# A second DMA queue for h and for zeros and scales, and a rank for bank copies, in a fused int4 FFN and S4 convolution kernel

## The chip, the cores and the metric

The kernel runs on one core of a Trainium2 chip. The metric is the device time of one execution in microseconds. Before the change three runs gave a median of 1330.53 us (1329.95 to 1332.14). The views quoted come from one profiled execution, which took 1331.74 us; its span, from the first instruction to the last, is 1330.0 us.

Engines are named as in the profile: PE multiplies matrices (PEld is its weight load), DVE and ACT work on vectors, POOL is the fourth compute engine, and SP here only issues transfers. SPq and POOLq are the queues in which those two engines hold their transfers: an engine takes its instructions in order, and an instruction that waits holds all behind it.

## The reference

x is 2048 x 1024. It is normalised row by row to xn, and the output is x plus two branches of xn:

```
xn  = (x - mean) / sqrt(var + 1e-5)
y   = irfft(rfft(xn, 2L) * rfft(K, 2L))[:L] + D * xn     # a causal convolution, L = 1024
g, u = xn @ Wg.T, xn @ Wu.T                              # 2752 columns each
h   = silu(g) * u
out = x + y + h @ Wd.T
```

Wg, Wu and Wd are held as 4-bit values, two to a byte, with a scale and a zero for each group of 64 along the input: w = (q - zero) * scale. K is the kernel of a state space model with 64 states, computed from its coefficients.

## The kernel before

All products are made in fp16 pairs: a float32 value is split into a high and a low half, and three of the four products of halves are taken. On top of that, the FFN uses a seven-product scheme in place of eight for a 2 x 2 block product: sums and differences of blocks are formed first, seven block products are made, and results are combined.

**First part (to about 145 us).** The rows are loaded, normalised, turned and combined; weights for the first column tiles are prepared by hand order (`pin`).

**Gate/up loop (about 145 to 875 us).** j runs over column tiles of 128 (j from 2 to 20 here), cp over two halves of the rows; `gate_up(j, cp, ...)` is one *unit*. A unit is seven products of 12 matmuls each into four PSUM banks A, B, C and D. Between products a bank's contents are copied or added on. ACT copies A to B (line 619), C to hb, B to D and C to ha, and makes the two silus; DVE adds D to hb and B to ha, and multiplies ha and hb by the silus. Three of the seven products of a unit (`fifth`, `fourth`, `third`, kept in `pending`) run inside the next unit. Tags limit buffers: banks A and C share four, B and D have two each, h tiles have four each for even j and for odd j.

`finish_h` stores h to DRAM (HF) as seven sums: of an even j it stores ha and keeps both halves; of the following odd j it stores both halves and forms and stores s4, s2, s5 (in s0's place) and s6. Each store is 256 KB, by SP. For the last j, h is split into halves and sent to HPL, from where the second stage reads it.

In the same loop weights are made ready, and this work is traced ahead of a unit or between units:

- `load_w` (two granules for each j, prepared a j ahead): raw values and scales by SP; unpack on DVE; `scale_c` (line 320), three short POOL operations on the scales; 16 ACTIVATEs on ACT that apply scale and zero; four sums on DVE (`sums`); high halves on ACT, low halves on DVE (both `nat`); two transposing transfers into `wf`, issued by SP (`w_t`, line 403). `wf` has four buffers, two for each j.
- `load_wd` (line 461), a generator that is stepped four times after every unit: the down weights, in ten rounds u of two granules ga and gb. `fetch_wd` loads raw values, spreads the transposed zeros and scales (SZT) over a factor tile `w` of two buffers by four transfers of 64 partitions each on SP (line 480), and has the raw values transposed. `dequant` (line 489) subtracts and multiplies on DVE; sums, high halves and low halves (`nd`) follow, and SP stores them to WD.

What orders the work: the Tile framework's planner orders each engine's instructions when the kernel is built. It simulates the program with its own durations, and among the instructions that are ready in the simulation it takes the one traced first; `tc.high_priority(n)` lets what is traced in its block count as if traced n instructions earlier. `tc.issue_after(ins)` puts what is traced in its block behind `ins` on the same engine. `tails` holds one DVE instruction for each finished unit, and `lag` counts them; the first dequant of a round is put behind the last of them (line 519), the second (line 533) is not. On the chip the order is fixed: an engine that waits for a late transfer doesn't pass on to the next instruction.

**Second stage (from about 875 us).** The convolution's products, and then the down product from HF and WD, whose results are added into the output by accumulating transfers from POOL's queue (line 1261).

Of the kernel before, what the change touches and what calls it, by code (L numbers as in the profile page):

```python
# [24 lines left out]
F16 = mybir.dt.float16  # L25
# [4 lines left out]
ALU = mybir.AluOpType  # L30
# [3 lines left out]
P = 128  # L34
# [4 lines left out]
NJ = 21  # L39
N_GRAN = 2 * NJ + 1 + 2 * NPAIR + 2  # L40
G_MIX = 2 * NJ
G_WD = G_MIX + 1
# [12 lines left out]
HS = 4.0  # L55
# [32 lines left out]
def build(nc, tc, x, xp, raw_d, sz_d, par_d, vct_d, tab_d, csrow_d, out):  # L88
# [3 lines left out]
    with es:  # L92
# [8 lines left out]
        HF = [dr.tile([7, P, NPAIR, 512], F32, name=f"HF{c}") for c in range(2)]  # L101
        HPL = [dr.tile([P, 2, 3, 512], F16, name=f"HPL{c}") for c in range(2)]
        WD2 = [dr.tile([7, P, NPAIR // 2, 2, 2, P], F16, name=f"WD{m}") for m in range(1, 8)]
        SZT = dr.tile([2 * NPAIR, 2, 2, 8, P], F32, name="SZT")
# [3 lines left out]
        def htile(name, tag="h"):  # L108
            return pools["h"].tile([P, 512], F32, tag=tag, name=name)
# [28 lines left out]
        def wtemp(kind, shape, dtype, name):  # L138
            return home[kind].tile(shape, dtype, tag=kind, name=name, **({"bufs": szbufs[0]} if kind == "sz" else {}))
# [14 lines left out]
        def split(dst, src):  # L154

            A.copy(dst[:, 0], src)
            V.tensor_tensor(dst[:, 1], src, dst[:, 0], ALU.subtract)
# [130 lines left out]
        with ea:  # L288
# [172 lines left out]
            def load_wd(u):  # L461


                pr, kq = divmod(u, 2)
                ga, gb = (G_WD + 2 * p + kq for p in (pr, pr + NPAIR // 2))
                tt, sub = V.tensor_tensor, ALU.subtract

                def load(gi):
                    raw = rawd[gi] = wtemp("raw", [P, 16, 32], I32, f"raw{gi}")
                    SP.dma_start(raw, raw_d[gi].rearrange("p (a b) -> p a b", a=16))  # L470

                def fetch_wd(gi):


                    raw = rawd.pop(gi)
                    w = wtemp("wd", [P, 8, 256], F32, f"w{gi}")
                    for i in range(2):
                        for b in range(2):
                            SP.dma_start(w[64 * b : 64 * b + 64, 4 * i : 4 * i + 4].rearrange("p f c -> p (f c)"),
                                         SZT[gi - G_WD, 1 - i, b].rearrange("c h -> (c h)").partition_broadcast(64))  # L480
                    q = wtemp("raw", [P, 16, 2, 32], I16, f"qn{gi}")
                    low = raw.bitcast(I16).rearrange("p a (b c) -> p a b c", c=2)[:, :, :, 0]
                    V.tensor_scalar(q[:, :, 0, :], low, 4, 15, ALU.logical_shift_right, ALU.bitwise_and)
                    V.tensor_scalar(q[:, :, 1, :], low, 15, None, ALU.bitwise_and)
                    qt = raw.bitcast(I16).rearrange("p a b -> p (a b)").rearrange("p (a b) -> p a b", a=8)
                    SP.dma_start_transpose(qt, q.rearrange("p a b c -> p (a b c)"))
                    return w, qt

                def dequant(w, qt):
                    x4 = w[:, 0:4]  # L490
                    tt(x4, qt.rearrange("p (f a) b -> p f (a b)", f=4), x4, sub)
                    tt(x4, x4, w[:, 4:8], ALU.mult)

                blocks = lambda w: w.rearrange("p f (m c) -> p f m c", m=2)
                nats = {}

                def hi(i, src):
                    nats[i] = wtemp("nat", [P, 7, 2, P], F16, f"nd{u}_{i}")
                    A.copy(nats[i][:, :, 0], src)

                def lo(i, src):
                    nat = nats.pop(i)
                    tt(nat[:, :, 1], src, nat[:, :, 0], sub)
                    SP.dma_start(
                        WD2[i - 1][:, :, pr, kq].rearrange("f p a c -> p f (a c)"), nat.rearrange("p f a c -> p f (a c)")
                    )

                nxt = [G_WD + 2 * ((u + 1) // 2 + o) + (u + 1) % 2 for o in (0, NPAIR // 2)] if u + 1 < NPAIR else None
                if u == 0:
                    load(ga)  # L510
                    load(gb)
                    yield from lag()
                    ready_wd[ga] = fetch_wd(ga)
                    yield
                ready_wd[gb] = fetch_wd(gb)
                yield from lag(2 if u == 0 else 1)
                ma = ready_wd.pop(ga)
                with tc.issue_after(tails[-1].ins):
                    dequant(*ma)
                wa = blocks(ma[0][:, 0:7])  # L520
                yield
                sums(ma[0], True)
                hi(1, wa[:, :, 0])
                yield
                if nxt:
                    load(nxt[0])
                lo(1, wa[:, :, 0])
                tt(wa[:, :, 0], wa[:, :, 1], wa[:, :, 0], sub)
                hi(5, wa[:, :, 0])
                yield  # L530
                lo(5, wa[:, :, 0])
                mb = ready_wd.pop(gb)
                dequant(*mb)
                wb = blocks(mb[0][:, 0:7])
                yield
                sums(mb[0], True)
                hi(3, wb[:, :, 1])
                tt(wa[:, :, 1], wb[:, :, 1], wa[:, :, 1], sub)
                yield
                if nxt:  # L540
                    load(nxt[1])
                lo(3, wb[:, :, 1])
                hi(7, wa[:, :, 1])
                tt(wb[:, :, 1], wb[:, :, 1], wa[:, :, 0], sub)
                yield

                lo(7, wa[:, :, 1])
                hi(6, wb[:, :, 1])
                if nxt:
                    ready_wd[nxt[0]] = fetch_wd(nxt[0])  # L550
                yield
                hi(2, wb[:, :, 0])
                lo(6, wb[:, :, 1])
                yield
                lo(2, wb[:, :, 0])
                tt(wb[:, :, 0], wb[:, :, 0], wb[:, :, 1], sub)
                hi(4, wb[:, :, 0])
                yield
                lo(4, wb[:, :, 0])
                yield  # L560
# [33 lines left out]

            pending = []

            def gate_up(j, cp, wf):

                def prod(i, ps, start, stop):
# [16 lines left out]
                add, mult = ALU.add, ALU.mult  # L616
                bA, bB = bank("A" + nm), bank("B" + nm, "B")
                prod(1, bA, True, True)
                heads[j, cp] = A.copy(bB, bA)
                rest(0)  # L620
                bC = bank("C" + nm)
                prod(7, bC, True, True)
                tag = "h" if j % 2 else "e"
                hb = htile("hb_" + nm, tag)
                A.copy(hb, bC)
                rest(1)
                prod(6, bB, False, True)
                bD = bank("D" + nm, "D")
                A.copy(bD, bB)
                prod(2, bA, False, True)  # L630
                A.activation(bA, bA, AF.Silu, scale=isc)
                rest(2)

                def fifth():
                    prod(5, bD, False, True)
                    tails.append(V.tensor_tensor(hb, bD, hb, add))

                def fourth():
                    prod(4, bC, False, True)
                    ha = htile("ha_" + nm, tag)  # L640
                    A.copy(ha, bC)
                    V.tensor_tensor(ha, bB, ha, add)
                    V.scalar_tensor_tensor(ha, ha, HS * isc, bA, mult, mult)
                    pending[2] = lambda: third(ha)

                def third(ha):
                    prod(3, bD, False, True)
                    A.activation(bD, bD, AF.Silu, scale=isc)
                    V.scalar_tensor_tensor(hb, hb, HS * isc, bD, mult, mult)
                    finish_h(j, cp, ha, hb)  # L650

                pending[:] = [fifth, fourth, None]

# [16 lines left out]
                V.scalar_tensor_tensor(h, bu, HS * isc, h, ALU.mult, ALU.mult)  # L670
                return h

            def finish_h(j, cp, ha, hb):
                nm = f"{j}_{cp}"
                if j == NJ - 1:
                    for c, h in enumerate((ha, hb)):
                        pc = wtemp("nat", [P, 2, 512], F16, f"hpl{nm}_{c}")
                        split(pc, h)
                        A.dma_start(HPL[cp][:, c, 0:2, :], pc)
                    return  # L680
                def emit(f, src):
                    SP.dma_start(HF[cp][f, :, j // 2, :], src)

                if j % 2 == 0:
                    emit(0, ha)
                    slots[cp] = (ha, hb)
                    return
                s0, s2 = slots.pop(cp)
                s1, s3 = ha, hb
                s4, s6 = (htile(f"s{n}_{nm}") for n in (4, 6))  # L690
                emit(1, s1)
                emit(3, s3)
                V.tensor_tensor(s4, s0, s2, ALU.subtract)
                emit(4, s4)
                V.tensor_tensor(s2, s2, s3, ALU.add)
                emit(2, s2)
                V.tensor_tensor(s0, s2, s0, ALU.subtract)
                emit(5, s0)
                V.tensor_tensor(s6, s1, s0, ALU.subtract)
                emit(6, s6)  # L700


            s4p = cst.tile([P, 208], F32, name="s4p")
# [705 lines left out]
```

## Time and profile before

| What | us |
|---|---|
| median of three runs | 1330.53 |
| profiled execution | 1331.74 |
| its span | 1330.0 |
| PE busy | 1274.0 |
| DVE busy | 987.9 |
| ACT busy | 669.2 |
| POOL busy | 182.8 |

Busy PE counts matmuls whose ends are modelled, 512 columns being issued every 0.216 us at full clock. In a group's row the numbers after the bar are busy time, mean ns of one, and the engine's idle time just before them with what ended it. In the list of waits the numbers are total us, how many waits, and the longest. A window's row gives busy times in a stretch and the clock that the throttle granted PE.

### The profile page before, as it was taken

Reading aid. Unit: us, or ns where it says so; the run is one execution under the profiler, and the core shown is the slowest. Engines: PE = TensorE matmul, PEld = TensorE weight load, DVE = VectorE, ACT = ScalarE, POOL = GpSimd, SP = SyncE. Lnnn points to the kernel's source line nnn. Section 1 sums busy time; section 2 is a strip of 40 time slices with the busy share of each in tenths; the row PEclk is TensorE's granted clock in tenths of the full one; section 3 lists DMA queues with packets and bytes.
Section 4 is the critical chain, followed back from the end, with each engine's and each line's share of the span. In section 5 each row is a group of like instructions: output and inputs, shape, how many; then the busy total and the mean of one; then the engine's idle time right before and its main releaser. Section 6 shows DMA issues by size and latency. Waiting matters only on the chain. (4 is left out here: it accounts for less than half of the span.)

```text
span 1330.0 us, 20904 instructions
## 1 busy us (share of the span) xinstructions
PE 1274.0 (96%) x7880; PEld 751.9 (57%) x7880; DVE 987.9 (74%) x1344; ACT 669.2 (50%) x1208; POOL 182.8 (14%) x267
## 2 busy tenths in 40 slices
PE   5999899999999899989989998999999999999998
PEld 5644344444444344444444443456558888888887
DVE  6779967486886877786878777462738898779792
ACT  4867566656656474766568475420204433443330
POOL 3230001010100000000111000000000032256440
PEclk8999899999999999999999998999999999999999
DMA  6791958469887988888798887765837779799981
GB/s 225 173 218 31 196 152 186 97 163 251 212 229 159 240 217 207 223 210 232 191 264 224 216 215 180 216 213 187 333 122 292 273 202 265 238 262 274 285 181 48
DMA packets 358401, 276.04 MB, mean 208 GB/s; under 512 B 211668, under 2 KB 304668, under 8 KB 354204
## 3 DMA queue, kind: packets, MB, share of 16 engines
q1 hardware_dynamic: 335676, 261.59, 70.6%
q0 software_dynamic: 21760, 10.49, 6.6%
q10 hardware_dynamic: 864, 2.62, 0.5%
q8 instruction: 62, 1.02, 0.3%
q14 instruction: 39, 0.32, 0.1%
HBM read 132.36 MB, written 94.84 MB: 171 GB/s over the span
## 5 line engine op out<-in xcount | busy, mean ns | idle before, releaser
L77 PEld LDWEIGHTS <-wf 128*128 128x128 f16 x3960 | 375.7, 99 | 467.8 <-issue 45.2
L77 PEld LDWEIGHTS <-g 128*128 128x128 f16 x2940 | 287.6, 98 | 33.5 <-issue 0.2
L77 ACT ACTIVATE w<-w,sz 128x64 f32<-128x64 int32 x640 | 217.9, 427 | 74.9 <-DVE w L77 58.3
L77 PE MATMUL A<-x,wf 128*128 128x512 f16 x912 | 215.2, 385 | 13.4 <-ACT ha L77 5.3
L77 PE MATMUL D<-x,wf 128*128 128x512 f16 x912 | 211.5, 380 | 14.1 <-DVE hb L77 12.1
L77 PE MATMUL C<-x,wf 128*128 128x512 f16 x912 | 208.0, 381 | 2.8 <-DVE ha L77 2.6
L77 ACT CAST g<-a 128x2560 f16<-128x2560 f32 x42 | 97.5, 2324 | 182.1 <-PE cv L77 52.6
L77 PE MATMUL A<-b,g 128*128 128x256 f16 x1680 | 185.9, 273 | 0.0
L77 DVE TENSOR_TENSOR w<-w 128x256 f32<-128x256 f32 (+2 forms) x272 | 136.9, 527 | 61.2 <-ACT w L77 54.7
L77 DVE TENSOR_TENSOR g<-a,g 128x2560 f16<-128x2560 f32 x42 | 118.4, 2821 | 30.9 <-ACT g L77 30.9
L1261 POOL DMA_DIRECT2D out<-o x64 | 78.8, 2139 | 360.7 <-DVE o L77 348.2
L322 POOL TENSOR_SCALAR sz<-sz 128x16 f32<-128x16 f32 x42 | 18.6, 443 | 673.2 <-DMA sz<-in_sz 622.7
L77 PE MATMUL B<-x,wf 128*128 128x512 f16 x456 | 106.7, 384 | 1.8 <-ACT B L77 1.8
L77 ACT CAST nat<-w 128x896 f16<-128x896 f32 x76 | 68.3, 935 | 72.9 <-issue 34.4
L77 ACT CAST nd<-w 128x896 f16<-128x896 f32 x70 | 64.1, 933 | 68.9 <-DVE w L77 47.6
L77 DVE TENSOR_TENSOR nat<-w,nat 128x896 f16<-128x896 f32 x76 | 81.0, 1087 | 19.3 <-ACT nat L77 19.1
L77 PE MATMUL D<-b,g 128*128 128x256 f16 x840 | 94.0, 273 | 0.0
L77 DVE TENSOR_TENSOR nd<-w,nd 128x896 f16<-128x896 f32 x70 | 75.5, 1086 | 16.3 <-ACT nd L77 16.0
L77 PEld LDWEIGHTS <-x 128*128 128x128 f16 x576 | 52.4, 98 | 23.7 <-issue 2.7
L77 DVE SCALAR_TENSOR_TENSOR p<-cv,p 128x512 f32<-128x512 f32 x32 | 21.9, 688 | 50.3 <-PE cv L77 44.9
L77 PE MATMUL cv<-band,x 128*128 128x512 f16 (+3 forms) x384 | 57.1, 299 | 0.0
L77 PE MATMUL g<-x,wf 128*128 128x128 f16 (+1 forms) x336 | 48.8, 293 | 1.7 <-ACT wf L82 0.8
(145 smaller groups left out, 1203.8 us busy)
## 6 DMA issues: line engine op xcount, KB each, us to landing
a<-HF SPq DMA_DIRECT2D x28, 1280.0 KB, 8.1
WD<-nd SPq DMA_DIRECT2D x70, 448.0 KB, 4.4
b<-WD SPq DMA_DIRECT2D x49, 640.0 KB, 5.9
w<-SZT SPq DMA_DIRECT2D x80, 256.0 KB, 5.7
raw<-in_raw SPq DMA_DIRECT2D x65, 256.0 KB, 3.8
HF<-ha SPq DMA_DIRECT2D x54, 256.0 KB, 2.9
HF<-s SPq DMA_DIRECT2D x40, 256.0 KB, 3.0
HF<-hb SPq DMA_DIRECT2D x36, 256.0 KB, 3.6
```

The lines of the kernel that those rows point to most:

```text
L77: return method(*args, **kw)
L322: G.tensor_scalar(sz[:, 0], sz[:, 0], WS, None, ALU.mult)
L1261: G.dma_start(dst, o[:, q], accum_op=ALU.add)
```

## The change

Three things are done.

1. The four SZT transfers of `fetch_wd` and all HF stores are issued by POOL (G) where SP issued them.
2. The four bank copies of a unit and the two sums (hb, ha) are traced under `tc.high_priority(400)`. The silus and the multiplications are not.
3. `tails` now holds the last multiplication of hb (in `third`) where it held the sum of hb (in `fifth`), and the second dequant of a round is put behind the last of `tails`, as the first one was.

Along with it `finish_h` is cut in two: what needs ha alone is sent right after ha is made, in `fourth`; s4 is formed in the even unit; and for the last j the ha half is split and sent before hb is made. The early columns (j of 0 and 1) still call `finish_h`, which calls both halves; their stores go to POOL as well.

```diff
-                            SP.dma_start(w[64 * b : 64 * b + 64, 4 * i : 4 * i + 4].rearrange("p f c -> p (f c)"),
-                                         SZT[gi - G_WD, 1 - i, b].rearrange("c h -> (c h)").partition_broadcast(64))
+                            G.dma_start(w[64 * b : 64 * b + 64, 4 * i : 4 * i + 4].rearrange("p f c -> p (f c)"),
+                                        SZT[gi - G_WD, 1 - i, b].rearrange("c h -> (c h)").partition_broadcast(64))
...
                 mb = ready_wd.pop(gb)
-                dequant(*mb)
+                with tc.issue_after(tails[-1].ins):
+                    dequant(*mb)
...
+            soon = lambda: tc.high_priority(400)
...
-                heads[j, cp] = A.copy(bB, bA)
+                with soon():
+                    heads[j, cp] = A.copy(bB, bA)
...
-                A.copy(hb, bC)
+                with soon():
+                    A.copy(hb, bC)
...
-                A.copy(bD, bB)
+                with soon():
+                    A.copy(bD, bB)
...
                 def fifth():
                     prod(5, bD, False, True)
-                    tails.append(V.tensor_tensor(hb, bD, hb, add))
+                    with soon():
+                        V.tensor_tensor(hb, bD, hb, add)
 
                 def fourth():
                     prod(4, bC, False, True)
                     ha = htile("ha_" + nm, tag)
-                    A.copy(ha, bC)
-                    V.tensor_tensor(ha, bB, ha, add)
+                    with soon():
+                        A.copy(ha, bC)
+                        V.tensor_tensor(ha, bB, ha, add)
                     V.scalar_tensor_tensor(ha, ha, HS * isc, bA, mult, mult)
+                    finish_ha(j, cp, ha)
                     pending[2] = lambda: third(ha)
 
                 def third(ha):
                     prod(3, bD, False, True)
                     A.activation(bD, bD, AF.Silu, scale=isc)
-                    V.scalar_tensor_tensor(hb, hb, HS * isc, bD, mult, mult)
-                    finish_h(j, cp, ha, hb)
+                    tails.append(V.scalar_tensor_tensor(hb, hb, HS * isc, bD, mult, mult))
+                    finish_hb(j, cp, ha, hb)
...
+            def emit(cp, j, f, src):
+                G.dma_start(HF[cp][f, :, j // 2, :], src)
+
+            def finish_ha(j, cp, ha):
+                if j == NJ - 1:
+                    return last_h(j, cp, 0, ha)
+                emit(cp, j, j % 2, ha)
+
+            def last_h(j, cp, c, h):
+                pc = wtemp("nat", [P, 2, 512], F16, f"hpl{j}_{cp}_{c}")
+                split(pc, h)
+                A.dma_start(HPL[cp][:, c, 0:2, :], pc)
+
+            def finish_hb(j, cp, ha, hb):
...
+                    return last_h(j, cp, 1, hb)
...
-                    emit(0, ha)
+                    s4 = htile(f"s4_{nm}")
+                    V.tensor_tensor(s4, ha, hb, ALU.subtract)
+                    emit(cp, j, 4, s4)
                     slots[cp] = (ha, hb)
                     return
                 s0, s2 = slots.pop(cp)
...
+                emit(cp, j, 3, hb)
+                V.tensor_tensor(s2, s2, hb, ALU.add)
+                emit(cp, j, 2, s2)
                 V.tensor_tensor(s0, s2, s0, ALU.subtract)
...
+            def finish_h(j, cp, ha, hb):
+                finish_ha(j, cp, ha)
+                finish_hb(j, cp, ha, hb)
```

More of the change, by code (lines that the diff above doesn't have):

```diff
@@ L671, in gate_up_plain @@
                 return h
-            def finish_h(j, cp, ha, hb):
+            def emit(cp, j, f, src):
[9 more added lines that the diff above has]
+            def finish_hb(j, cp, ha, hb):
                 nm = f"{j}_{cp}"
                 if j == NJ - 1:
[L676 to L682, printed above, removed]
+                    return last_h(j, cp, 1, hb)
                 if j % 2 == 0:
-                    emit(0, ha)
+                    s4 = htile(f"s4_{nm}")
+                    V.tensor_tensor(s4, ha, hb, ALU.subtract)
+                    emit(cp, j, 4, s4)
                     slots[cp] = (ha, hb)
@@ L688, in finish_h @@
                 s0, s2 = slots.pop(cp)
[L689 to L696, printed above, removed]
-                V.tensor_tensor(s0, s2, s0, ALU.subtract)
-                emit(5, s0)
-                V.tensor_tensor(s6, s1, s0, ALU.subtract)
-                emit(6, s6)
+                emit(cp, j, 3, hb)
+                V.tensor_tensor(s2, s2, hb, ALU.add)
+                emit(cp, j, 2, s2)
+                V.tensor_tensor(s0, s2, s0, ALU.subtract)
+                emit(cp, j, 5, s0)
+                s6 = htile(f"s6_{nm}")
+                V.tensor_tensor(s6, ha, s0, ALU.subtract)
+                emit(cp, j, 6, s6)
+            def finish_h(j, cp, ha, hb):
+                finish_ha(j, cp, ha)
+                finish_hb(j, cp, ha, hb)
             s4p = cst.tile([P, 208], F32, name="s4p")
```

## The prediction

> **What bounds the kernel now.** I read the page first, parts 1 and 2:
>
> ```profile
> span 1330.0 us, 20904 instructions
> ...
> PE 1274.0 (96%) x7880; PEld 751.9 (57%) x7880; DVE 987.9 (74%) x1344; ACT 669.2 (50%) x1208; POOL 182.8 (14%) x267
> ...
> PEclk8999899999999999999999998999999999999999
> ```
>
> PE is busy 96% of the span, so only its idle time and its stretches at a low clock can be won. The table of windows says where they lie:
>
> ```profile
> 450.00:600.00 150.00, 137.81 (x655) 62.75 (x654) 124.99 (x231) 89.86 (x194) 10.23 (x24) 1.00 0.85 211
> 600.00:750.00 150.00, 142.84 (x653) 63.73 (x652) 111.61 (x183) 96.44 (x209) 14.97 (x21) 0.99 0.89 226
> 750.00:875.00 125.00, 118.52 (x536) 53.05 (x535) 81.67 (x122) 68.95 (x144) 3.94 (x12) 0.97 0.75 201
> 875.00:1330.00 455.00, 449.40 (x3788) 363.54 (x3786) 327.80 (x268) 130.47 (x79) 98.41 (x80) 1.00 0.77 229
> ```
>
> The columns after the length are busy PE, PEld, DVE, ACT, POOL, then clock, DMA share and GB/s. From 450 to 875 us PE idles 12.2 + 7.2 + 6.5 = 25.8 us. After 875 us it idles only at the very end, which this change doesn't reach. So the stage is the gate/up loop, and I asked PE's waits between 145 and 880 us:
>
> ```profile
> PE D L77 <- DVE hb L77: 12.1, 4, 5.5
> PE A L77 <- ACT ha L77: 5.3, 3, 3.0
> PE A L77 <- DVE ha L77: 3.7, 3, 1.9
> PE C L77 <- DVE ha L77: 2.6, 3, 1.8
> PE s4s L77 <- ACT ha L77: 2.5, 2, 1.6
> PE D L77 <- ACT D L77: 2.0, 1, 2.0
> PE B L77 <- ACT B L77: 1.8, 3, 0.7
> ```
>
> With 0.3 us for hb's copy that is 30.3 us, all for a bank that ACT or DVE had not emptied. The weights (wf) cost 0.8 us there. The largest wait, seen in the timeline:
>
> ```profile
> 796.76 3.17 SPq L77 DMA_DIRECT2D w<-SZT  x4
> ...
> 803.71 1.23 DVE L77 TENSOR_TENSOR w<-raw,w 128x1024 f32<-128x1024 int16 x1 [8.28 <-DMA w<-SZT]
> 804.86 0.68 DVE L77 TENSOR_TENSOR hb<-D,hb 128x512 f32<-128x512 f32 x1
> ...
> 805.59 1.86 PE L77 MATMUL D<-x,wf 128*128 128x512 f16 x4 [5.46 <-DVE hb L77]
> ```
>
> DVE stood idle 8.28 us for a weight factor, with the 0.68 us sum that PE needed queued behind. DVE was late by order, not by load. Low clock adds to it: the four D matmuls take 1.86 us here, twelve take 2.75 us at full clock. By the trace's clock records PE ran at half clock from 340.1 to 343.5, 620.0 to 623.4 and 804.3 to 811.1 us, each beside such a gap; half of the part with work is 1.7 + 1.7 + 2.8 = 6.2 us. Prize: 36.5 us.
>
> **1, the rank of copies and sums.** Nothing is added; four copies and two sums a unit come ahead of weight work in ACT's and DVE's order. The offset of 400 covers a whole j: I count 168 matmuls, about 20 bank operations, 13 h stores and sums, 66 weight instructions of two granules, some 55 of the down weights and s4, about 320. So they also pass weight work traced at the head of the same j. In the case above the hb sum could have run near 795 us, when its bank was full; third's product wanted it at 800.1. Against 12.1 us of hb waits I credit 11. Of the ACT waits and copies (5.3 + 2.5 + 2.0 + 1.8 + 0.3 = 11.9) I credit 9: the two silus stay unranked. Of the ha waits on DVE (6.3) only 2.5, since ha's last multiplication, which frees bank A, stays unranked. Sum 22.5. Of the clock, the stretches at 620 and 804 us go with their gaps: 4 of 4.5.
>
> **2, the second granule's dequant behind a unit's sums, and the mark moved** from the sum of hb to its last multiplication. It adds order, no work. Both dequants (2 x 1.22 us) start up to three products (3 x 2.59 us) later. Cover: the last store of down weights is issued at 844.8 us, the first load of them at 878.4. Without that cover up to 8 us would go to the head of the second stage. I take nothing.
>
> **3, DMAs from SP to POOL.** 140 HF stores and 80 factor loads. SP's issue of one is 0.38 and 0.61 us at the median: SP sheds 140 x 0.38 + 80 x 0.61 = 102 us. POOL has no plain store in this trace; its rows are the accumulating ones:
>
> ```profile
> L1261 POOL DMA_DIRECT2D out<-o x64 | 78.8, 2139 | 360.7 <-DVE o L77 348.2
> ```
>
> and the list of DMA issues (KB each, median us from issue to landing):
>
> ```profile
> w<-SZT SPq DMA_DIRECT2D x80, 256.0 KB, 5.7
> ...
> HF<-ha SPq DMA_DIRECT2D x54, 256.0 KB, 2.9
> ...
> out<-o POOLq DMA_DIRECT2D x64, 128.0 KB, 10.5
> ...
> out<-U POOLq DMA_DIRECT2D x16, 128.0 KB, 6.4
> ```
>
> Bounds for one issue: 0.38 (SP) and 2.14 us (out<-o); out<-U, the same kind on POOL, has 1.87, which I take as the nearest row. 220 x 1.87 = 411 us of POOL, between 84 and 471, in a loop where it is busy under 15 us in 150. There is room, but four factor loads now take 7.5 us to issue instead of 3.2. For landing the bounds are 2.9 and 10.5 us; I take 6.4.
>
> What waits: POOL's queue holds an HF store until DVE has written h, and behind it stand scale_c (three short operations, then 16 ACTIVATEs of 0.43 us on ACT) and the next factor loads. ACT already waited 13.5 us for scale_c, three times. I add 3 us to PE. An h buffer is free later by 6.4 − 2.9 = 3.5 us; ACT's hb copy waited 6.0 us for that in four places. The ranked copies stand in front of weight work, so PE sees little: 2 us. Odd units take three new h buffers where they took four, since s4 moves to the even unit: no price, bounds −2 to 0.
>
> In return SP is free for weight transposes. They were in time by little: four started at 735.0 and were issued by 746.4, with 4.6 us to landing, for a product at 752.2, so 1 to 3 us. Weight work that is now passed over can miss this: 4 us, bounds 0 and 12 (about 17 j, 0.7 us each). Before 145 us, 14 stores join POOL's small norm operations: 0, bounds −2 and 3.
>
> **Two rules weighed.** The Trainium skill, "DMA: Bandwidth & Descriptors", section "Issuing engines are not separate DMA queues", speaks against part 3: a second queue saves only issue time, usually small. The trace differs where SP's queue was blocked, not slow: in the loop it waited 127.0 us for DVE's w operations. By the page alone part 3 would give 0.
>
> The skill's "SBUF — State Buffer", the box on the "DVE blocks DMA" trap, says GpSimd can't write descriptors while DVE runs in a two-port mode, and gives 620 ns alone and 3100 beside it. In this trace scale_c's last operation has a median of 254 ns and a maximum of 3545, which would fit; the page's 3.1 us an issue would be an estimate of 682 us of POOL, nearly the whole loop, and would make the slow rival likely.
>
> **Sum.** −22.5 − 4 + 3 + 2 + 4 = −17.5 us. The profiled execution took 1331.74 us (span 1330.0 and 1.7 around it), 1.2 over the median of 1330.53. 1331.74 − 17.5 = 1314.2, less 1.2: 1313.
>
> **Rivals.**
>
> A, nearly all goes (chance 0.08): 36.5 less at most 5 of new waits, 1294 to 1299. For it: the waits are short and the sums had idle DVE time. Against: DVE is busy 125.0 of 150 us from 450 to 600.
>
> B, weights become the bound (0.24): ranking delays the chain unpack, ACTIVATE, sums, halves, transpose, and the wait moves from bank to wf. The 4 us become 12: −26.5 + 3 + 2 + 12 = −9.5, 1321; with the credits cut to 17 as well, 1330.5. For it: the 1 to 3 us of margin. Against: SP is freer.
>
> C, slower (0.24): factor loads through POOL land late, and DVE stands at a dequant with everything behind it. Today 32.9 us of such waits cost PE the hb gaps at 453, 690 and 805 us (11.5) and 2.8 of clock: 0.43 us for each. 20 dequants that wait 5 us each cost 43; less today's 14.3 and 12 from the other copies, +17: 1347. It decides from 61 us of such waits, 3 us a dequant against 1.6 now. For it: 7.5 us of issue, stores ahead in the queue, landing up to 10.5. Against: on SP the loads stood behind other waits; in the case shown a load of raw, one of sz and two stores held SP from 792.1 to 796.7.
>
> D, the change doesn't do what it says: the copies stay behind weight work, since what was ready first in the planner's time went first anyway. Then only part 3 acts: 0 to +5, 1330.5 to 1335.5; I count it in B and C.
>
> **Numbers.** Forecast 1304 to 1320: 0.44; A 0.08; B 0.24, of it 0.14 below 1327.9; C 0.24. A measurement of this kernel can tell about 0.2%, 2.7 us. Faster 0.44 + 0.08 + 0.14 = 0.66; same 0.10; slower 0.24. The range leaves out the far ends of A and C: 1297 to 1340.
>
> **What would show it.** Right: PE's waits for hb and ha under 10 us in sum, no half clock after 300 us, DVE's wait for w<-SZT without a PE gap behind it. Part 3 right: POOL's issues under 2.1 us each, HF landing under 6.4. Wrong: wf waits over 5 us (B); w<-SZT waits over 61 us, or ACT waiting for sz over 40 us (C). The prediction fails most easily by POOL's cost, for which there is no row of a plain store.

## The result and the profile after

The changed kernel takes 1375.7 us (median of four runs, 1374.5 to 1378.4) where the kernel before took 1331.3 in the same runs (1330.0 to 1332.9): a ratio of 1.0336, 95% interval 1.0316 to 1.0356. It is slower by 44 us, where 18 less were forecast. The profiled execution took 1376.05 us. Its page begins:

```profile
span 1374.1 us, 21058 instructions
...
PE 1289.2 (94%) x7880; PEld 753.5 (55%) x7880; DVE 987.8 (72%) x1344; ACT 671.8 (49%) x1208; POOL 303.3 (22%) x487
...
PEclk9999999999999999998999999999999999999999
```

PE does the same 7880 matmuls but is busy 15.2 us longer: more of them ran at a lower clock. DVE and ACT have the same work as before, POOL has 120 us more. The windows, with the columns as before, place the loss:

```profile
450.00:600.00 150.00, 135.47 (x629) 60.63 (x628) 114.89 (x193) 81.89 (x176) 35.56 (x68) 0.98 0.90 207
600.00:750.00 150.00, 125.18 (x551) 54.12 (x550) 96.25 (x177) 78.59 (x172) 30.18 (x58) 0.94 0.90 185
750.00:900.00 150.00, 138.66 (x611) 60.78 (x611) 109.53 (x171) 91.45 (x193) 33.10 (x60) 0.96 0.84 202
900.00:1375.00 475.00, 469.82 (x3883) 372.79 (x3881) 337.07 (x281) 141.83 (x105) 99.11 (x85) 1.00 0.78 231
```

The loop is the place again: from 600 to 750 us PE gets 551 matmuls done where it did 653, idles 24.8 us where it idled 7.2, and the granted clock falls to 0.94. In that stretch the 16 DMA engines are busy the same share, 0.89 before and 0.90 now, but move 185 GB/s where they moved 226. The second stage is untouched. PE's waits in the loop (140 to 930 us; total, times, longest):

```profile
PE A L77 <- DMA wf<-nat: 39.1, 18, 6.8
PE D L77 <- DVE hb L77: 10.1, 3, 7.0
PE A L77 <- ACT ha L77: 4.9, 3, 2.7
PE D L77 <- ACT D L77: 3.8, 2, 2.3
```

The wait for weights, under 1 us in the stretch shown before, is now the largest by far; the bank waits shrank a little. One case of it, in the timeline:

```profile
660.72 4.06 SPq L77 DMA_TRANSPOSE wf<-nat  x2
...
662.96 2.11 POOL L479 DMA_DIRECT2D w<-SZT  x4 [2.19 <-DVE nd L77]
...
673.52 1.03 PE L77 MATMUL A<-x,wf 128*128 128x512 f16 x2 [6.83 <-DMA wf<-nat]
```

SP issues a pair of weight transposes from 660.7 us on, POOL issues four factor loads beside them at 663.0, and PE, which needs the weights, can start only at 673.5, after 6.83 us of waiting and 12.8 us after the first transpose. The view of the weight tile shows the 76 transposes of the loop, first before the change and then after it: how long SP took to issue one (ns, min/median/max), and the time from the start of the issue to the landing, as far as the trace tells it (for 41 of them before, 49 after):

```profile
L77 SPq DMA_TRANSPOSE wf<-nat x76: 1369/2060/3708, 130.5 to 820.9; - x76
...
DMA to landing us min/median/max: 4.0/4.6/6.4
```

```profile
L77 SPq DMA_TRANSPOSE wf<-nat x76: 1370/2501/15082, 123.5 to 879.5; - x76
...
DMA to landing us min/median/max: 4.0/4.9/24.1
```

So after the change some transposes land late, and SP itself is held up for as long as 15.1 us in issuing one. Sorted by what the trace shows in flight, after the change, from 150 to 900 us: transposes with neither factor loads nor HF stores beside them land in 4.6 us on average (4 of them), with HF stores alone in 5.4 (24), with factor loads in 9.3 (16). A single landing can be put down to the wrong transfer, so the experiments below go by PE's waits and by times.

The bill, from 120 to 930 us: PE idles 40.4 us for weights and 24.3 for banks (before 4.2 and 30.9), 29.6 us more. It runs 54.6 us at half clock where it ran 20.5; half of the difference is 17. Together 47, for 44 measured.

### The profile page after: what moved, and what is told of

It reads as the page before. It is cut to its first block, busy times and chain, and to the rows that moved or that the text cites. A ratio compares the mean times of both kernels' runs of the same rounds, so it can differ in the third digit from the quotient of the medians.

```text
span 1374.1 us, 21058 instructions
## 1 busy us (share of the span) xinstructions
PE 1289.2 (94%) x7880; PEld 753.5 (55%) x7880; DVE 987.8 (72%) x1344; ACT 671.8 (49%) x1208; POOL 303.3 (22%) x487
## 3 DMA queue, kind: packets, MB, share of 16 engines
q0 software_dynamic: 39360, 68.18, 21.4%
## 4 chain that ended last, share of the span: by engine, by line
PE 42%; DMA 5%; issue 2%; DVE 1%; ACT 1%; POOL 1%; ACTq 0%; DVEq 0%; POOLq 0%; SPq 0%
PE A L77 16%; PE D L77 9%; PE cv L77 8%; PE E L77 3%; PE C L77 3%; DMA wf<-nat 2%; PE B L77 1%; DMA sz<-in_sz 1%; DMA w<-SZT 1%; ACT w L77 1%; PE cc L77 1%; DVE w L77 1%; DMA hpl<-HPL 0%; POOL sz L322 0%; DVE nat L77 0%
## 5 line engine op out<-in xcount | busy, mean ns | idle before, releaser
L77 PE MATMUL A<-x,wf 128*128 128x512 f16 x912 | 221.8, 388 | 47.6 <-DMA wf<-nat 40.4
L77 PE MATMUL D<-x,wf 128*128 128x512 f16 x912 | 221.9, 392 | 13.9 <-DVE hb L77 10.1
L77 PE MATMUL C<-x,wf 128*128 128x512 f16 x912 | 211.3, 383 | 1.1 <-DVE x L82 1.1
L77 DVE TENSOR_TENSOR g<-a,g 128x2560 f16<-128x2560 f32 x42 | 118.5, 2823 | 30.9 <-ACT g L77 30.9
L77 ACT CAST nat<-w 128x896 f16<-128x896 f32 x76 | 68.0, 935 | 50.9 <-DVE w L77 27.9
L77 DVE TENSOR_TENSOR nd<-w,nd 128x896 f16<-128x896 f32 x70 | 75.8, 1087 | 17.5 <-ACT nd L77 17.4
L77 DVE SCALAR_TENSOR_TENSOR p<-cv,p 128x512 f32<-128x512 f32 x32 | 22.0, 689 | 49.8 <-PE cv L77 48.0
L479 POOL DMA_DIRECT2D w<-SZT x80 | 42.1, 535 | 55.6 <-issue 28.8
```

Of the source, the lines that this page charges most:

```text
L77: return method(*args, **kw)
L479: G.dma_start(w[64 * b : 64 * b + 64, 4 * i : 4 * i + 4].rearrange("p f c -> p (f c)"), SZT[gi - G_WD, 1 - i, b].rearrange("c h -> (c h)") ...
```

## The experiments

Each was timed beside the kernel before, except the two probes. The table gives median, ratio with 95% interval, and from the profile between 120 and 930 us: PE's idle time for weights / for banks (every wait but those for weights), DVE's waits for factors (w<-SZT), ACT's waits for an HF store to free an h buffer, and time at half clock, all in us ("–": not taken).

| kernel | us | ratio | PE: weights / banks | SZT | HF | half clock |
|---|---|---|---|---|---|---|
| before | 1331.3 | 1 | 4.2 / 30.9 | 32.9 | 7.1 | 20.5 |
| after | 1375.7 | 1.0336 (1.0316–1.0356) | 40.4 / 24.3 | 24.8 | 45.8 | 54.6 |
| a_szt_sp | 1337.7 | 1.0020 (1.0000–1.0040) | 22.6 / 17.5 | 18.7 | 46.7 | 34.1 |
| a_hf_sp | 1354.6 | 1.0170 (1.0140–1.0199) | 39.3 / 12.2 | 22.9 | 12.1 | 41.0 |
| a_both_sp | 1321.6 | 0.9921 (0.9898–0.9944) | 21.4 / 6.8 | 14.0 | 10.4 | 6.8 |
| a_szt_act | 1378.8 | 1.0355 (1.0328–1.0382) | 65.6 / 7.1 | 50.0 | – | – |
| b_szt_pool | 1349.1 | 1.0118 (1.0098–1.0137) | 5.6 / 40.2 | 28.5 | 21.6 | 37.5 |
| b_hf_pool | 1347.8 | 1.0115 (1.0096–1.0134) | 4.9 / 41.2 | 35.2 | 14.1 | 41.0 |
| a_norank | 1376.6 | 1.0317 (1.0280–1.0354) | 39.8 / 28.7 | 25.4 | 47.7 | – |
| a_noord | 1364.0 | 1.0235 (1.0207–1.0264) | 9.9 / 50.9 | 49.8 | 16.3 | 41.0 |
| b_rank | 1335.2 | 1.0024 (1.0010–1.0037) | 5.5 / 30.6 | 37.2 | 8.3 | – |
| b_order | 1316.7 | 0.9872 (0.9848–0.9896) | 15.0 / 9.0 | 12.8 | 18.2 | 10.2 |
| c_mark | 1333.5 | 1.0002 (0.9986–1.0017) | 15.3 / 22.3 | 33.0 | – | – |
| c_behind | 1331.3 | 0.9976 (0.9959–0.9993) | 8.4 / 28.7 | 32.0 | – | – |
| c_ro | 1321.0 | 0.9912 (0.9892–0.9933) | 15.0 / 11.2 | 15.2 | – | – |
| c_os | 1318.8 | 0.9907 (0.9876–0.9938) | 19.3 / 4.8 | 14.2 | – | – |
| c_rs | 1336.8 | 1.0026 (1.0017–1.0036) | 5.8 / 28.9 | 34.1 | – | – |
| d_whl | 1325.3 | 0.9947 (0.9928–0.9967) | 18.5 / 9.1 | 20.8 | – | – |

### Which transfers cost: the moves undone, one by one

**a_szt_sp**: after, with the factor loads back on SP.

```diff
-                            G.dma_start(w[64 * b : 64 * b + 64, 4 * i : 4 * i + 4].rearrange("p f c -> p (f c)"),
+                            SP.dma_start(w[64 * b : 64 * b + 64, 4 * i : 4 * i + 4].rearrange("p f c -> p (f c)"),
```

> The changed kernel with the four factor loads of a granule (w<-SZT) back on SP; HF stores stay on POOL, rank and order stay. Transfer theory (factor loads on a second queue run beside the weight transposes and slow them: in the changed kernel a transpose with factor loads in flight landed after 9.3 us in the mean, without any POOL transfer after 4.6): PE's wf waits fall from 39.1 to under 15 us, transposes land within 6.5 us, time 1335 to 1352. Rank theory (weight work that is passed over is late whatever the queue): wf waits stay over 28 us, time 1362 to 1378. Buffer theory (HF stores through POOL keep h buffers and hold ACT): ACT's waits for HF (45.8 us) stay, time 1362 to 1378.

**a_hf_sp**: after, with the HF stores back on SP. **a_both_sp**: both back on SP, so that rank, order and the cut of `finish_h` remain.

```diff
-                G.dma_start(HF[cp][f, :, j // 2, :], src)
+                SP.dma_start(HF[cp][f, :, j // 2, :], src)
```

> The changed kernel with the HF stores back on SP; factor loads stay on POOL, rank and order stay. Buffer theory: ACT's waits for HF stores fall from 45.8 to under 10 us and the wf waits with them, time 1335 to 1352. Transfer theory: transposes still land late beside factor loads, wf waits over 25 us, time 1360 to 1378. Rank theory: 1362 to 1378, or later still, since SP has the stores again in front of its transposes.

> The changed kernel with factor loads and HF stores both back on SP: what is left is the rank, the order of the second dequant, and finish_h in two halves. Transfer theory (both kinds of POOL transfers slow the transposes or hold ACT): the two single steps back gave -38 and -21 us; with both, wf waits under 12 us, no ACT waits for HF over 12 us, and the rank can pay: 1312 to 1328. Planner theory (each new plan of this loop is as good or bad as chance makes it, and the order and rank gain nothing): 1330 to 1350, wf waits of 15 us or more.

Taking back the factor loads gains 38.0 us, the stores 21.1, both 54.1. The four times nearly add: from 1321.6, stores on POOL cost 16.1 us, factor loads 33.0, both 54.1, which is 5 more than the sum. The ten runs of a_szt_sp spread from 1330.6 to 1341.1 us, so the single costs are rough. Part 3 is the whole loss, and what is left of the change is faster than before by 9.7 us of the medians. Not all came as expected: a_szt_sp and a_both_sp have the times of the transfer theory, but more weight waits (22.6 where it gave under 15, 21.4 where it gave under 12), and a_hf_sp lies between the ranges of its theories. The table shows two roads: factor loads on POOL raise the weight wait (21.4 to 39.3), and stores on POOL raise the time that ACT waits for an h buffer (10.4 to 46.7). In the kernel after those waits are:

```profile
ACT ha L77 <- DMA HF<-hb: 30.5, 7, 13.1
ACT hb L77 <- DMA HF<-hb: 15.3, 5, 9.2
```

POOL's queue holds a store until DVE has its h, 71.7 to 88.7 us in all for each of ha, hb and the sums. What stands behind it, the next store among it, goes later; that this makes ACT's waits is my reading. Without part 2 (a_noord) the same stores on POOL cost ACT only 16.3 us.

The weight wait has two sources, and the queues are one of them. With all transfers on SP there is still

```profile
PE A L77 <- DMA wf<-nat: 21.4, 21, 4.4
```

in a_both_sp, against 4.2 us before. The trace allows an estimate: of each wait I count as late landing what lies beyond 4.7 us after the start of the last transpose's issue (4.7 is the average landing before). Then 19.7 of the 40.4 us after are late landing, and the other 20.7 are transposes that were issued late. In a_both_sp the two are 2.9 and 18.5. So the moves add the late landing, and the lateness of the issue is there without them; b_order below, with 15.0 us, puts most of it down to part 2.

### The moves made alone on the kernel before

**b_szt_pool** and **b_hf_pool**: one word each, `SP.dma_start` to `G.dma_start`, at the factor loads or at the HF stores of before.

> The kernel before with the 80 factor loads on POOL's queue and nothing else changed. Transfer theory: transposes with factor loads in flight land after 7 to 10 us against 4.7, wf waits rise from 4.2 to 15 to 35 us, time 1350 to 1372. If the loss of the changed kernel comes only from the parts together: 1325 to 1338.

> The kernel before with the HF stores on POOL's queue and nothing else changed. Buffer theory: ACT's waits for HF rise from 7.1 to 25 to 50 us, transposes beside HF stores land some 0.7 to 1.5 us later, time 1338 to 1356. If stores on POOL cost nothing by themselves: 1325 to 1336.

Alone they cost 1.18% and 1.15%, some 15 us each. Here the loss shows in another place: PE waits 10 us more for banks and hardly more for weights, and loses 8 to 10 us to the half clock (half of 17.0 and 20.5). ACT waits longer for HF stores in both (7.1 to 21.6 and 14.1). How these bank waits arise I did not isolate: each edit also makes the planner arrange the loop anew. Both waits that had been expected stayed away: 5.6 us for weights where the transfer theory gave 15 to 35, and 14.1 for HF stores where the buffer theory gave 25 to 50.

### POOL, or any second queue?

**a_szt_act**: after, with the factor loads issued by ACT (`G.dma_start` to `A.dma_start`).

> The changed kernel with the factor loads on ACT's own hardware queue in place of POOL's. Transfer theory (any second queue beside the transposes delays them): transposes with factor loads in flight land after 7 to 10 us on average against 4.7 without, wf waits over 25 us, 1360 to 1390. If POOL's software queue is the trouble: transposes land within 6 us, 1335 to 1352.

1378.8 us, no better than POOL, and weights are later still:

```profile
PE A L77 <- DMA wf<-nat: 63.5, 23, 10.7
```

By the count above 44.1 of the 65.6 us from 120 us on are late landing. So it isn't POOL, nor the way in which POOL issues. **probe** takes the transfers out of the kernel: phases of 12 weight transposes (SP) with 12 factor loads or HF stores of the kernel's sizes beside them on some queue. It leaves out the kernel's whole computation.

> A kernel that leaves out all of the reference's work and copies x to the output after ten phases that are separated by waits: 12 weight transposes (the wf form, fp16, 128 x 1792) on SP twice alone; then 12 factor loads (64 partitions, 4 KB row, 256 KB) alone on SP and alone on POOL; then 12 transposes together with 12 factor loads on SP's own queue (one before each), on POOL's queue, on ACT's queue; then with 12 HF stores (128 x 2 KB) on POOL, on SP; last 12 HF stores alone on POOL. Transfer theory: a transpose alone takes about 1.4 to 2.1 us of SP and lands within 5 us; with POOL loads beside it the phase is longer than the two alone one after the other, or the transposes land two times later than with the same loads on SP. If only bandwidth counts: the phases with loads on SP, POOL and ACT are equally long within 10%. If the loss was all in the plan: transposes beside POOL loads land no later than alone.

The windows of three phases (length, busy DVE and POOL, clock, DMA share, GB/s): transposes alone, transposes with factor loads on POOL, transposes with HF stores on SP between them:

```profile
20.80:48.70 27.90, 0.31 (x6) 0.00 (x0) 1.00 1.06 197
142.80:189.90 47.10, 0.45 (x6) 6.10 (x12) 1.00 1.09 184
286.20:324.50 38.30, 0.00 (x0) 0.00 (x0) 1.00 1.08 227
```

Twelve transposes alone keep all 16 DMA engines busy (a share of 1.06). Factor loads beside them add 19.2 us from POOL and 25.1 from ACT (53.0). What a second queue changes is who goes first. From POOL all loads had landed 25.6 us into the phase; the second transpose, which alone landed 6.4 us into its phase, landed at 26.2. SP was held up meanwhile: issuing that second transpose took 14.46 us, where it takes about 2.1 alone. With stores on POOL the second transpose landed at 18.7 us, and the slowest landing with stores on SP took 4.83. The timeline above shows such a late landing in the kernel. Phases of loads alone ran into each other here; the phase with loads on SP's own queue began beside the last of them and took 41.8 us, and after its second transpose none took over 5.2 us to land.

**probe2** separates them, with four of each, again without the kernel's computation.

> A kernel that leaves out all of the reference's work and copies x to the output after fifteen phases, each kept from the next by waits: four weight transposes alone (twice), four factor loads alone on SP, on POOL, on ACT; then four loads and four transposes: loads first on SP, transposes first on SP, loads on POOL, loads on ACT; four HF stores alone on SP and POOL, and four with four transposes: first on SP, last on SP, on POOL; the phase with loads on POOL once more. Transfer theory, as the first such kernel's rows read (12 transposes alone 27.9 us, beside 12 loads on POOL 47.1 us, one of them landing after 24.9 us): a second queue adds no bandwidth, so a phase takes about the sum of its parts wherever the loads are queued, but the last transpose lands soonest when the transposes stand first on SP (about 10 us after the phase starts), and with loads on POOL or ACT as late as when the loads stand first on SP (15 to 20 us). If POOL's queue by itself is the trouble: later with POOL than with ACT by over 3 us. If neither: within 2 us of transposes alone.

Four transposes alone take 10.6 us, four factor loads alone 6.8 on SP, 6.9 on POOL and 6.9 on ACT. Together they take 15.9 on SP, 15.7 with POOL and 16.0 with ACT: the parts nearly add whatever the queue. But loads and transposes hardly met here: on all three queues the first transpose began some 5 us after the first load, so these sums say little, and the late landing beside loads wasn't tested again. The stores on POOL did meet the transposes: 4.1 us alone on SP and 4.8 on POOL, with transposes 13.2 and 14.4, and beside those of POOL the second transpose took 8.7 us to land, against 4.9 alone. That a second queue adds no bandwidth rests on the first probe: twelve transposes at 27.9 us and three times four loads at 6.9 make 48.6, an estimate; the phase with loads on POOL took 47.1, the one with loads on ACT 53.0.

### Rank and order

**a_norank**: after, without the ranks. **b_rank**: before, with the ranks alone.

```diff
-            soon = lambda: tc.high_priority(400)
+            soon = lambda: nullcontext()
```

> The changed kernel without the rank: copies and sums count as where they are traced; queues and order stay. Rank theory: wf waits fall under 12 us, waits for hb and ha come back at 20 to 30 us, time 1335 to 1352. Transfer theory: wf waits stay at 30 to 45 us and bank waits are added, time 1370 to 1400. Buffer theory: 1370 to 1400 as well, with ACT's waits for HF unchanged.

> The kernel before with the rank of 400 for the four copies and two sums and nothing else changed (queues, marks and finish_h as before). The prediction's first step: bank waits fall from 31 to under 14 us, time 1305 to 1320. If the rank is no gain since a kernel without it and one with it differ by nothing (1376.6 against 1375.7 us in the changed kernel): bank waits 22 to 35 us, 1326 to 1338. If it delays weights: wf waits over 15 us, 1340 to 1352.

Rank gains nothing in either place: 1376.6 against 1375.7 without and with it, and 1.0024 on the kernel before, if anything slower. Laid beside before's in the order of the trace (tile names without buffer numbers), b_rank's instructions differ in 24 of 1208 places on ACT and in 100 of 1344 on DVE; with order alone 433 and 732 differ.

**a_noord**: after, without part 2. **b_order**: before, with part 2 alone.

```diff
-                dequant(*mb)
+                with tc.issue_after(tails[-1].ins):
+                    dequant(*mb)
...
-                    tails.append(V.tensor_tensor(hb, bD, hb, add))
+                    V.tensor_tensor(hb, bD, hb, add)
...
-                    V.scalar_tensor_tensor(hb, hb, HS * isc, bD, mult, mult)
+                    tails.append(V.scalar_tensor_tensor(hb, hb, HS * isc, bD, mult, mult))
```

> The changed kernel with the old mark (tails holds the sum of hb) and the second dequant free; queues and rank stay. If the later dequant is what delays weights: wf waits under 15 us, time 1335 to 1352. Transfer, rank and buffer theories: 1366 to 1382, wf waits over 28 us; a free dequant may stand before a sum again, +0 to +6.

> The kernel before with the order part alone: second dequant behind the last mark, mark moved to hb's last multiplication; no rank, finish_h whole, all transfers on SP. If the order alone carries the gain that rank and order gave together (1321.0): 1316 to 1324, bank waits under 14 us. If it needs the rank or the cut finish_h: 1326 to 1338.

Order alone gives 1316.7 us, the fastest version of all and faster than both kernels. Its PE waits (145 to 880 us), and its DVE waits for factors:

```profile
PE A L77 <- DMA wf<-nat: 11.1, 10, 2.2
PE B L77 <- ACT B L77: 5.5, 2, 3.0
...
PE D L77 <- DVE hb L77: 0.6, 1, 0.6
```

```profile
DVE w L77 <- DMA w<-SZT: 12.8, 8, 3.6
```

The 12.1 us for hb are gone, and DVE's waits for factors fall from 32.9 to 12.8. The bill closes: 11.1 us less of idle PE and half of 10.3 us of half clock are 16.3, for 14.6 by the medians (17 by the ratio). In the kernel after the same part does harm (a_noord is 11.7 us faster than after): with it weights are late (40.4 against 9.9), without it banks (50.9 against 24.3). This bill closes too: 3.9 us less of idle PE and half of 13.7 us of half clock are 10.7. The weight wait of a_noord is the one that its first theory gave, its time is neither's. And the transposes land there no earlier than in the kernel after:

```profile
DMA to landing us min/median/max: 4.0/5.6/21.1
```

By the count above only 5.3 us of that reach PE, against 19.7. So late landing alone does not make the weight wait. It takes part 2 as well, with which the transposes have little time in hand: 13.4 of the 15.0 us in b_order are late issue, where before has 3.9.

**c_mark** moves the mark alone (the last two edits above); **c_behind** puts the second dequant behind the old mark alone (the first).

> The kernel before with the moved mark alone: tails holds hb's last multiplication, so the first dequant stands later; the second dequant stays free. If the gain comes from the second dequant no longer standing with its wait for w<-SZT in front of a sum: no gain here, 1328 to 1340, bank waits over 24 us. If it comes from the first dequant's later place: 1316 to 1325.

> The kernel before with the second dequant behind the old mark (the sum of hb of the unit before), mark not moved. If holding the second dequant back is the cause: 1316 to 1325, DVE's waits for w<-SZT under 20 us, bank waits under 16 us. If the mark is: 1328 to 1338.

1.0002 and 0.9976. Neither half has more than a fifth of the gain, and DVE's factor waits stay at 33.0 and 32.0: only the two together bring these down. Each half alone also takes PE's wait for hb from 12.1 to 0.7 us, and gains nothing by it, since other waits come instead (15.3 / 22.3 and 8.4 / 28.7). So the gain isn't the hb wait alone. What b_order, c_ro, c_os and a_both_sp share is the factor wait of DVE, 12.8 to 15.2 us, against 32.0 to 37.2 in all kernels with transfers on SP that lack a half of part 2. Why it takes both halves stays open.

**c_ro** (rank and order), **c_os** (order and the cut of `finish_h` into `finish_ha` and `finish_hb`) and **c_rs** (rank and the cut), all on before with all transfers on SP.

> Queues and finish_h as before; rank and order of the second dequant (with the moved mark) on. Rank alone gave +2.9 us, rank, order and the cut finish_h together -10.7. If the order is what lets the rank pay, since DVE no longer stands at a dequant in front of a sum: 1316 to 1326, bank waits under 14 us. If the cut finish_h is: 1330 to 1338, bank waits over 22 us.

> Queues as before; order of the second dequant and the cut finish_h on, no rank. If the rank has a part of the gain: 1326 to 1338 and bank waits over 18 us. If the rank has none: 1317 to 1326.

> Queues and dequants as before; rank and the cut finish_h on. If the cut is what lets the rank pay (s4 formed in the even unit, one h buffer less for odd units): 1316 to 1326, bank waits under 14 us. If the order is: 1330 to 1338, DVE's waits for w<-SZT over 25 us and bank waits over 22 us.

The three with order lie at 1318.8 to 1321.6 (a_both_sp has all three parts), the one without at 1336.8. Rank beside order: 1321.0 against 1316.7; rank beside order and the cut: 1321.6 against 1318.8. It never gains. I read nothing into differences of 2 to 4 us: any small edit rearranges the plan by as much.

**d_whl**: b_order, with the weight halves and transposes ranked, to get at the 15 us of weight waits left.

```diff
-                w_hi(gi)
-                w_lo(gi)
-                w_t(gi)
+                with tc.high_priority(400):
+                    w_hi(gi)
+                    w_lo(gi)
+                    w_t(gi)
```

> The fastest version so far (the order part alone, 1316.7 us) with the high and low halves of the gate/up weights and their transposes ranked 400 earlier. If its remaining 15.0 us of wf waits come from weight work that is planned too late: wf waits under 8 us, 1306 to 1313. If they come from when a wf buffer is free and SP's transposes (2 us each): wf waits 11 to 18 us, 1313 to 1322.

1325.3 us, 8.6 slower than b_order, with the weight wait no smaller (18.5). A miss; what those waits hang on stays open.

## Why the prediction was wrong, point by point

**The stage and the wait it started from** were right: all that the change did happened in the gate/up loop, and in the case shown the hb wait did come from DVE standing at a dequant for its factors.

**Part 1, the rank: −22.5 us credited, nothing measured.** This step failed. In the case shown, the hb sum stood behind a dequant that waited. The prediction gave the cure to rank, but rank only says who goes first among instructions that are ready in the planner's simulation, and the late transfer is late only on the chip. Rival D had said this in words ("what was ready first in the planner's time went first anyway") and was given no chance of its own. In b_rank PE waits 8.2 us for hb, less than before, but 30.6 for all banks against 30.9. That the order hardly moved on ACT and DVE is seen; that the planner's durations are the reason is argued.

**Part 2, the order: costed at nothing, measured −1.28% (0.9872).** The second failed step. The dequant that waits may no longer stand in front of that unit's sum; in b_order PE's wait for hb falls to 0.6 us and DVE's for factors by 20.1. It also has a price that the prediction left out: the weight wait goes from 4.2 to 15.0. "It adds order, no work" was true and beside the point. The clock went with the gaps as forecast: half clock 20.5 to 10.2 us in b_order.

**Part 3, the queues: +9 us taken (3 + 2 + 4), some +54 measured.** This step decides the sign. (The 54 hold beside part 2; beside rank and cut alone both moves cost 27, 1364.0 against 1336.8, and each alone on before some 15.) Term by term:

- POOL's issue was taken at 1.87 us (0.38 to 2.14). In the kernel after a factor load and a store have a median near 0.52 and 0.55 us: 220 of them are about 120 us of POOL, not 411. Far too dear, and of no account.
- Landing was taken at 6.4 us. The list of DMA issues after gives 7.0 for factor loads and 3.9 to 4.6 for stores:

```profile
w<-SZT POOLq DMA_DIRECT2D x80, 256.0 KB, 7.0
HF<-ha POOLq DMA_DIRECT2D x54, 256.0 KB, 3.9
HF<-s POOLq DMA_DIRECT2D x40, 256.0 KB, 4.6
```

- h buffers: 2 us allowed, since an ACT wait "PE sees little". ACT's waits for them went from 7.1 to 45.8 us, and the stores' move costs 16 us.
- Weights: 4 us, at most 12, because passed-over weight work might come late. The wait grew by 36.2 us: 17.2 with all transfers on SP (a_both_sp), which the prediction would have laid to the rank and which come with the order (5.5 us in b_rank, 15.0 in b_order), and 19.0 with the moves. For these it had no term: transposes and loads share the DMA engines, and the windows showed these busy 0.75 to 0.89 of the time. The margin of 1 to 3 us was misread as well, since the list counts a landing from the start of the issue: 743.1 + 4.6 leaves some 4 us to 752.2.
- "SP is free for weight transposes" was the argument against the Trainium skill, "DMA: Bandwidth & Descriptors", section "Issuing engines are not separate DMA queues", which says that transfers started by different engines end on the same 16 DMA engines and that only issue time is saved. The runs agree with the page: 47.1 us with loads on POOL and 53.0 with loads on ACT, against an estimate of 48.6 for the parts one after the other. "By the page alone part 3 would give 0" left out who goes first: loads from the second queue ran in front of the transposes.
- From the box on the "DVE blocks DMA" trap in the Trainium skill's "SBUF — State Buffer" the prediction made 3.1 us an issue. The two figures stand further down that page, in "A bandwidth-pool intuition that's wrong (but worth ruling out)", and are for a whole DMA. No issue of the 220 took over 1.28 us, with DVE busy 72% of the span, and the factor loads' median landing was 7.0 us from POOL and 7.2 from ACT, so no run here shows that trap.

**The rivals.** B named the wait that came (weights), at 12 us instead of 40, and by the rank, where the order and the moves made it. C named the sign and 1347 us, but by factor loads late at the dequants: DVE waited 24.8 us for them, less than before and far from the 61 at which C was to decide, and ACT waited 5.9 us for scales, not over 40. A slower kernel by the weights' road was on nobody's list.

**The signs set out beforehand.** Waits for hb and ha under 10 us: no, 17.2 (10.1 + 4.9, and 2.2 for ha on DVE). No half clock after 300 us: no, ten stretches. Part 3's own signs came true, with issues under 2.1 us and stores landing in 3.9 to 4.6 at the median, though part 3 made the loss: they watched the price of POOL and not the transposes. Wf waits over 5 us: yes, 39.1, and that sign alone pointed to the cause.

Settled: part 3 makes the loss, ACT's queue does it for the factor loads as POOL's does, and order, with both halves, makes what gain there is. Seen, but not taken apart: order, which gains 15 us with all transfers on SP, loses 12 with them on POOL; the counts of late landing say that the weights then have no time in hand. Open: how the moves alone on before turn into bank waits, and why order makes the transposes start later.

## What to carry to other kernels

Before a transfer is moved to another queue, look at the DMA share of that stage and at what is urgent on the queue it leaves. Where the engines are near full, as here, one queue's order can keep background loads behind the transfer that the critical engine needs, and a second queue lifts it. When an engine stands at a late transfer with urgent work behind it, put the waiting instruction behind that work in the written order; the rank changed little here. And time the parts of a bundled change one by one and in pairs: one part of this change, which lost 44 us, gains 15 alone and loses 12 beside another.

## What the runs showed of the hardware

- Twelve transposes of 128 x 1792 fp16 values fill all 16 DMA engines by themselves: 27.9 us, share 1.06, 197 GB/s. Beside them loads from POOL stretched a landing from 4.7 to 24.9 us at worst, loads from ACT to 22.7, and SP stood up to 14.46 us in issuing one transpose.
- A plain 256 KB transfer issued by POOL costs that engine about 0.54 us, where the accumulating one in the same kernel costs 2.1. Four such loads alone take 6.9 us from POOL and 6.8 from SP.
- Short gaps on PE cost more than themselves: with 29.6 us more of idle time in the loop came 34 us more at half clock, worth another 17.
